# A two-layer transformer block in fp32: ScalarE and GpSimd kept in the order of issue during attention, the settling of a chunk split into parts, and three PSUM banks of small pieces in one ring

## The chip, the cores and the metric

The kernel runs on one core of a Trainium2 chip. The metric is the time of one execution on the device, in microseconds. A core has five engines that run side by side, each with an instruction stream of its own: TensorE (PE in the profile; PEld is its loading of weights), VectorE (DVE), ScalarE (ACT), GpSimd (POOL) and SyncE (SP), which here only issues DMA transfers. GpSimd issues the indirect DMAs (gathers and scatters by a list of rows). Matmul results land in PSUM, which has eight banks of 128 x 512 fp32; everything else on the chip lies in SBUF. An engine takes its instructions in the order of its stream, and semaphores tell it when another engine's or a DMA's result is there.

## The reference, cut to what matters

Eight sequences of 256 tokens, 512 wide, all in fp32:

```
x  = hidden_states                                  # 8 x 256 x 512
xn = layernorm(x)
x  = x + lightning_attention(xn) + moe(xn)          # layer 0
xn = layernorm(x)
x  = x + softmax_attention(xn) + low_rank_moe(xn)   # layer 1

lightning_attention: qkv = silu(xn @ qkv_w.T), 32 heads of 128;
    scores = q k^T * decay (causal), o = scores v; o scaled by its RMS over all heads, times norm_w,
    gated by sigmoid(xn @ gate_w.T), then @ out_w.T
moe: 16 experts, the best 2 of each token (chosen in 2 of 4 groups), weighted by their scores,
    each silu(x w1 + b1) * (x w2 + b2) @ w3 + b3; two shared experts for every token
softmax_attention: one head of 128
low_rank_moe: 64 experts of rank 16, the best 16 of each token, gates by softmax
```

## The kernel before, in words

**Tiling.** The 2048 tokens are four chunks of 512 (NCH), each of four tiles of 128 tokens (TPC). All large products use a seven-product Strassen scheme (p1 to p7), with sums of weights and tokens made beforehand.

**The opening** normalizes, runs the shared experts, routes and lays out the slots of the chosen experts. It takes the first 195 us or so, and uses other functions than the ones changed.

**Attention.** In the pool `attn`, for each chunk i = 0 to 3 and each of eight groups of four heads g, the seven products of the scheme run one after another (`Outer`, L964, one for each of `plan`), and each of these is split by the same scheme once more: p1, p7, p3 of the Outer before, p6, p4, p2, p5. So a group makes 7 x 7 = 49 small products (in chunk 0, which also writes the weight sums for later, 7 x 8 without the inner saving). A group with its chunk is called a unit here; there are 32, and in the even stretch from 1529.12 to 1969.10 us six of them take 73.3 us each. One `product` (L662, its matmul is L667) is four matmuls into a quarter of a PSUM bank each, eight records in the trace. The banks of these products are ps_a (2), ps_b and ps_e. A finished bank is copied by ScalarE to cp (`copied`, L997), or combined by VectorE to r, c or a (`result`, through `tt`, L97); GpSimd adds r into c. When a quarter of a unit is complete, `Quarter.begin` books the small pieces that use it: silu of q and k (L745), the gate (L750 to L752), scores (L770, L771, into ps_sc), attend (L782, L783, into ps_o; squares for the RMS at L797; gated outputs gT at L802), and the output projection (L859, or `project_plain`, L879), whose results are added into acc.

**Slots.** After each product `slot()` (L680) takes the next piece that is due from a list; `later(n, f)` books a piece n slots ahead. One slot runs one piece, or two if more than twelve wait; pieces that give TensorE nothing to do are not counted.

**Experts.** In the units from the ninth on, `expert(j)` books 47 blocks of 128 expert slots, three to a unit for seven units and then two. Each starts with a load of its tokens by SP (xw from xd) and a gather of its weights by GpSimd (L698), and has turn (L707), up (L717, into ps_sc; h at L724, he at L725) and down (L729, into ps_y; copied to ye at L734, stored to yd) 8, 11 and 14 slots later. The tokens were scattered to xd (L1095) during chunk 0.

**Small PSUM pieces.** ps_sc has two banks that take turns, ps_y one bank, ps_o one. A piece can write a bank once the reader of what it last held is done.

**Settling.** `settle` (L552) brings a chunk from layer 0 to layer 1: for each of the two experts of a token it gathers four tiles of rows from yd (L559, GpSimd) and adds them, times the gate, into x (L566, VectorE), then normalizes (L231 to L236). Chunk 0 is settled at the unit before the last of chunk 3 (`wrapped_up`, L1146), the others in the tail.

**The tail.** Layer 1 runs for each chunk: low_rank(0) (L1416, matmuls at L1423) with the turning of the softmax and its product with v as fillers, settle of the next chunk, low_rank(2) with the attention output as filler (`attended`, L1465, into ps_y), then a last `seven` (L1493) with route, qk, values, softmax and gates of the next chunk's head as fillers, after turn_rows (L240).

**Who sets the order.** The program is traced in Python, and a scheduler of the language then orders the stream of each engine by priorities and its own estimates. So an instruction can run ahead of one that was traced before it, if no data stand against it.

Of the kernel before, what the change touches and what calls it, by code (L numbers as in the profile page):

```python
# [9 lines left out]
FP = mybir.dt.float32  # L10
# [8 lines left out]
P = 128  # L19
CH = 512  # L20
NCH = NT // CH
TPC = CH // P
# [11 lines left out]
TOP = 2  # L34
# [3 lines left out]
NSLOT = NMT * P  # L38
# [28 lines left out]
def block_kernel(  # L67
# [25 lines left out]
    nc = tc.nc  # L93
    mm = nc.tensor.matmul

    def tt(o, a, b, op, eng=None):
        (eng or nc.vector).tensor_tensor(o, a, b, op)  # L97
# [8 lines left out]
    ps = ctx.enter_context(tc.tile_pool(name="ps", bufs=1, space=PSUM))  # L106
# [21 lines left out]
        return stage.tile([P, C + WROW], FP, tag="xw", name=name)  # L128

    def ps_sc():  # L130
        return ps.tile([P, 512], FP, tag="sc", name="ps_sc", bufs=2)

    def ps_o():
        return ps.tile([P, 512], FP, tag="o", name="ps_o", bufs=1)

    def ps_y():
        return ps.tile([P, 512], FP, tag="y", name="ps_y", bufs=1)


    opening = ExitStack()  # L140
# [26 lines left out]
    for i in range(1, NCH):  # L167
# [8 lines left out]
    yd = dram.tile([NSLOT, C], FP, name="yd")  # L176
# [27 lines left out]
        out=before, in_=before, pattern=[[1, E], [-1, E]], compare_op=ALU.is_gt,  # L204
# [11 lines left out]
        out=dist[:, 0:S], in_=dist[:, 0:S], pattern=[[1, S]], compare_op=ALU.is_ge,  # L216
# [134 lines left out]
    def add(o, a, b, eng=None):  # L351
        tt(o, a, b, ALU.add, eng)
# [70 lines left out]
    for i in range(NCH):  # L423
# [23 lines left out]
    slots = const.tile([P, TOP, NTT], I32, name="slots")  # L447
    slot_gates = const.tile([P, TOP, NTT], FP, name="slot_gates")
# [6 lines left out]
        out=earlier, in_=earlier, pattern=[[1, P]], compare_op=ALU.is_gt,  # L455
# [25 lines left out]
    at = NTT * E  # L481
# [67 lines left out]
    settled = {}  # L549
    accs = []  # L550

    def settle(i, x_, spare):  # L552


        for n in range(TOP):
            y = spare()
            for t in range(TPC):
                at = i * TPC + t
                nc.gpsimd.indirect_dma_start(  # L559
                    out=y[:, t, :], out_offset=None, in_=yd[:, :],  # L560
                    in_offset=bass.IndirectOffsetOnAxis(ap=slots[:, n, at : at + 1], axis=0),
                    bounds_check=NSLOT - 1, oob_is_err=False,
                )
            for t in range(TPC):
                gate = slot_gates[:, n, i * TPC + t : i * TPC + t + 1]
                nc.vector.scalar_tensor_tensor(  # L566
                    x_[:, t, :], y[:, t, :], gate, x_[:, t, :], ALU.mult, ALU.add
                )
        xn = spare()
        normalize(xn, x_)  # L570
        return xn

    acc = {}

# [12 lines left out]
    def finish(i, r):  # L587

        for b in range(2):
            for t in range(2):  # L590
                n = 2 * b + t
                o = r[:, n, :].rearrange("p (h c) -> p h c", h=2)
                nc.vector.scalar_tensor_tensor(
                    o, acc[i][:, 2 * b : 2 * b + 2, t], all_rms[i][:, n : n + 1], o, ALU.mult, ALU.add
                )

    def spare8():
        return staged("spare")[:, 0 : TPC * C].rearrange("p (t c) -> p t c", t=TPC)

    with tc.tile_pool(name="attn", bufs=1) as attn:  # L600
        sums_ = {}


# [72 lines left out]
        def later(after, f):  # L676
            pieces.append((now[0] + after, len(pieces), f))
            pieces.sort(key=lambda x: x[:2])

        def slot():  # L680

            now[0] += 1
            n = 0
            while pieces and pieces[0][0] <= now[0] and n < (2 if len(pieces) > 12 else 1):
                f = pieces.pop(0)[2]
                f()
                n += getattr(f, "func", f).__name__ not in ("silu", "gate", "row", "scatter", "load_sum", "sums1", "sums2", "sums3", "sums4", "out_sum")


        class Expert:  # L690
# [270 lines left out]
        class Outer:  # L961
# [10 lines left out]
            x_ = {}  # L972
# [173 lines left out]
        def wrapped_up():  # L1146

            x_, y = spare8(), spare8()
            nc.sync.dma_start(out=x_, in_=xs_[0])
            accs.append(x_)  # L1150
            settled[0] = settle(0, x_, lambda: y)

        def prepare(n):
            if n < len(plan):
# [120 lines left out]
    def spare():  # L1275
        return work.tile([P, TPC, C], FP, tag="spare", name="spare")

    def next_x(i):
        x_ = spare8() if i % 2 == 0 else work.tile([P, TPC, C], FP, tag="x", name=f"x{i}", bufs=1)
        accs.append(x_)  # L1280
        if i + 1 < NCH:
            nc.sync.dma_start(out=x_, in_=xs_[i])
        else:
            nc.sync.dma_start(out=x_, in_=xr[i])
            finish(i, x_)
        return x_
# [104 lines left out]
    for i in range(NCH):  # L1391
# [24 lines left out]
        def low_rank(j, fill):  # L1416

            gates2 = [spread(h * HJ + j) for h in range(2)]

            def product(bank, w, xx, first):  # L1420
                for n in range(2):
                    for c in range(HC):
                        mm(  # L1423
                            bank[:, bass.ts(n, S)], w[:, c, bass.ts(j + n, P)], xx[:, c, :],
                            start=(first and n == 0 and c == 0), stop=(c == HC - 1),
                            skip_group_check=True,
                        )

            def out_(h, b, bank, c):
                o = hg[:, h * HJ + j : h * HJ + j + 2, bass.ts(b, S)]  # L1430
                if c is not None:
                    add(c, bank, c)
                    bank = c
                tt(o, bank.rearrange("p (n s) -> p n s", n=2), gates2[h][:, :, bass.ts(b, S)], ALU.mult)

            seven(work, product, WA, XA, out_, fill)
# [28 lines left out]
        def attended(t):  # L1465
# [2 lines left out]
            mm(py, oT[:, bass.ts(t, P)], wo_t, start=True, stop=True)  # L1468
            add(xc[:, t, :], py, xc[:, t, :])

        low_rank(0, {2: [partial(turned, 0)], 7: [partial(turned, 1)], 5: [partial(weighed, 0)], 3: [partial(weighed, 1)]})
        if i + 1 < NCH:
            settled[i + 1] = settle(i + 1, next_x(i + 1), spare)
        low_rank(2, {k: [partial(attended, t)] for t, k in enumerate((2, 7, 5, 3))})
        if i + 1 < NCH:
            if i % 2:
                yT1 = xT[0]
            else:
                yT1 = work.tile([P, NC, CH], FP, tag="yT", name=f"yT{i + 1}", bufs=1)
# [123 lines left out]
```

## Time and profile before

| | |
|---|---|
| median of 3 runs | 2904.78 us (2901.41 to 2913.6) |
| the profiled execution | 2910.55 us |
| its span | 2908.9 us |
| its mean granted TensorE clock | 0.989 |
| TensorE busy | 2811.0 us, 97% of the span |
| VectorE busy | 1553.3 us, 53% |
| ScalarE busy | 953.1 us, 33% |
| GpSimd busy | 1469.4 us, 51% |
| moved by DMA | 763.20 MB, 262 GB/s in the mean |

In stretches (the stage borders are rounded; busy time of TensorE, mean granted clock):

| stretch, us | what runs | PE busy, us | clock |
|---|---|---|---|
| 0 to 195 | opening | 167.31 | 0.92 |
| 195 to 850 | attention, chunk 0 | 639.66 | 0.99 |
| 850 to 1430 | chunk 1, experts | 568.44 | 1.00 |
| 1430 to 2021 | chunk 2, experts | 585.59 | 1.00 |
| 2021 to 2240 | chunk 3, last experts | 215.68 | 1.00 |
| 2240 to 2600 | chunk 3, chunk 0 settled | 342.26 | 0.98 |
| 2600 to 2909 | tail, layer 1 | 292.02 | 0.99 |

How to read a group or a wait: the line of the kernel, the engine, the operation, then output<-input by the program's names; ps_ names are PSUM banks. A wait names the instruction that stood still, what released it, the microseconds in total, how often and the longest. "c", "r", "acc" and other results of L97 come from one helper for all elementwise operations of two tensors, so they are told apart by name, not by line. A row of the timeline has start, length, engine, line, operation and, in brackets, how long the engine was idle before it and what ended that.

### The profile page before, as it was taken

How to read it: one execution, taken by the hardware profiler on the slowest of the kernel's cores; microseconds unless marked ns; L12 is line 12 of the kernel's file. 1: busy time of each engine (PE TensorE's matmuls, PEld its weight loads, DVE VectorE, ACT ScalarE, POOL GpSimd, SP SyncE). 2: the span in 40 equal slices, each digit the busy share in tenths (PEclk: the TensorE clock that was granted, in tenths of full speed). 3: DMA queues.
4: the chain of work that ended last, by engine and by line, in shares of the span. 5: the costliest groups of instructions: out<-in, count | busy, mean ns of one | idle time of the engine just before them, and what ended most of it. 6: DMA issues, size and time to landing. Idle time of an engine off the chain costs nothing.

```text
span 2908.9 us, 49460 instructions
## 1 busy us (share of the span) xinstructions
PE 2811.0 (97%) x19864; PEld 2570.9 (88%) x19864; DVE 1553.3 (53%) x2615; ACT 953.1 (33%) x1683; POOL 1469.4 (51%) x1213
## 2 busy tenths in 40 slices
PE   8989999999999999999999999999999989999999
PEld 4469999999989999999999999999999979987877
DVE  7555666666544545444545555555445455558463
ACT  3312222221244333333443333333433334332111
POOL 4535666565445555555645555445444665554110
PEclk9999999999999999999999999999999999999999
DMA  7788998888987777777777777777777776653111
GB/s 263 291 307 329 350 350 344 342 333 329 368 319 258 277 251 262 260 264 277 285 263 258 257 259 260 261 280 282 282 257 257 282 297 225 224 213 96 60 60 60
DMA packets 161942, 763.20 MB, mean 262 GB/s; under 512 B 18209, under 2 KB 24225, under 8 KB 109874
## 3 DMA queue, kind: packets, MB, share of 16 engines
q1 hardware_dynamic: 149826, 706.25, 65.7%
q0 software_dynamic: 11888, 53.79, 5.3%
q8 instruction: 157, 2.57, 0.4%
q14 instruction: 71, 0.58, 0.1%
HBM read 596.14 MB, written 163.05 MB: 261 GB/s over the span
## 4 chain that ended last, share of the span: by engine, by line
PE 78%; DVE 9%; DMA 4%; issue 4%; POOL 2%; ACT 1%; SPq 0%; DVEq 0%; POOLq 0%; ACTq 0%
PE ps_a L667 22%; PE ps_e L667 11%; PE ps_b L667 7%; PE ps_y L859 5%; PE ps_sc L859 4%; PE ps_o L782 3%; PE ps_sc L770 3%; PE ps_sc L717 2%; PE ps_y L879 2%; PE ps_sc L879 2%; DVE c L97 2%; PE ps_a L1493 2%; PE ps_o L783 2%; PE ps_sc L771 2%; PE ps_y L729 1%
## 5 line engine op out<-in xcount | busy, mean ns | idle before, releaser
L667 PE MATMUL ps_a<-xt,w 128*128 128x128 f32 x5376 | 752.9, 276 | 15.0 <-DVE r L97 7.4
L667 PEld LDWEIGHTS ps_a<-xt,w 128*128 128x128 f32 x5376 | 683.1, 193 | 36.4 <-issue 14.9
L97 POOL TENSOR_TENSOR c<-c,r 128x512 f32<-128x512 f32 x240 | 323.7, 1366 | 186.3 <-DVE r L97 138.7
L745 ACT ACTIVATE c<-c 128x512 f32<-128x512 f32 x256 | 161.3, 630 | 656.7 <-DVE c L97 360.2
L667 PE MATMUL ps_e<-xt,w 128*128 128x128 f32 x2688 | 374.3, 275 | 2.0 <-DVE c L97 1.3
L97 POOL TENSOR_TENSOR c<-c 128x512 f32<-128x512 f32 x216 | 270.7, 1269 | 184.6 <-DVE c L97 182.6
L97 POOL TENSOR_TENSOR w<-w 128x512 f32<-128x512 f32 x224 | 292.9, 1322 | 133.4 <-DVE w L97 67.8
L667 PEld LDWEIGHTS ps_e<-xt,w 128*128 128x128 f32 x2688 | 344.7, 192 | 12.4 <-issue 4.1
L97 POOL TENSOR_TENSOR sums<-sums,sq 128x512 f32<-128x512 f32 x120 | 154.3, 1286 | 386.5 <-ACT sq L797 386.1
L667 PE MATMUL ps_a<-w,xt 128*128 128x128 f32 x1792 | 346.9, 275 | 0.0
L997 ACT COPY cp<-ps_a 128x512 f32<-128x512 f32 x336 | 195.0, 580 | 426.9 <-PE ps_a L667 426.9
L667 PEld LDWEIGHTS ps_a<-w,xt 128*128 128x128 f32 x1792 | 272.6, 192 | 0.0
L97 DVE TENSOR_TENSOR c<-ps_a,c 128x512 f32<-128x512 f32 x232 | 158.0, 687 | 214.5 <-PE ps_a L667 213.5
L667 PE MATMUL ps_b<-xt,w 128*128 128x128 f32 x1680 | 236.3, 277 | 4.8 <-ACT c L1011 4.2
L802 DVE SCALAR_TENSOR_TENSOR gT<-ps_o,nw,c 128x256 f32<-128x256 f32 x256 | 111.9, 479 | 226.5 <-ACT sq L797 222.4
L667 PEld LDWEIGHTS ps_b<-xt,w 128*128 128x128 f32 x1680 | 216.9, 194 | 16.1 <-issue 5.5
L859 PE MATMUL ps_y<-wo,gT 128*128 128x256 f32 x736 | 175.4, 381 | 0.6 <-DVE acc L97 0.6
L667 PE MATMUL ps_e<-w,xt 128*128 128x128 f32 x896 | 173.5, 275 | 0.0
L770 PE MATMUL ps_sc<-c 128*128 128x256 f32 x512 | 154.1, 383 | 11.3 <-DVE he L725 7.7
L97 DVE TENSOR_TENSOR s<-ps_sc,decay 128x384 f32<-128x384 f32 x256 | 139.1, 551 | 39.0 <-PE ps_sc L771 37.7
L782 PE MATMUL ps_o<-s,c 128*128 128x256 f32 x512 | 153.8, 382 | 4.3 <-DVE s L97 4.2
L859 PEld LDWEIGHTS ps_y<-wo,gT 128*128 128x128 f32 x736 | 132.8, 190 | 15.5 <-issue 0.7
(307 smaller groups left out, 4768.1 us busy)
## 6 DMA issues: line engine op xcount, KB each, us to landing
w<-in_w_att_dram SPq DMA_DIRECT2D x128, 1024.0 KB
st<-in_w_att_dram SPq DMA_DIRECT2D x32, 1024.0 KB
wo<-in_w_out_dram SPq DMA_DIRECT2D x113, 256.0 KB
decay<-dec SPq DMA_DIRECT2D x64, 384.0 KB
w<-ws0p SPq DMA_DIRECT2D x12, 1792.0 KB
w<-ws1p SPq DMA_DIRECT2D x12, 1792.0 KB
w<-ws2p SPq DMA_DIRECT2D x12, 1792.0 KB
w<-ws3p SPq DMA_DIRECT2D x12, 1792.0 KB
```

Of the source, the lines that this page charges most:

```text
L97: (eng or nc.vector).tensor_tensor(o, a, b, op)
L667: mm(bank[:, bass.ts(ty, P)], a, b, start=(first and ty == 0), stop=True, skip_group_check=True,)
L717: mm(pu[:, bass.ts(n, P)], w12[:, n, c, :], self.xeT[:, c, :], start=(c == 0), stop=(c == NC - 1),)
L745: nc.scalar.activation(qk, qk, AF.Silu)
L770: mm(p[:, 0:S], self.c[:, 2 * hh, P : 2 * P], q, start=True, stop=True)
L771: mm(p[:, S : S + P], self.c[:, 2 * hh + 1, P : 2 * P], q[:, 1, :], start=True, stop=True,)
L782: mm(po[:, bass.ts(hh, S)], v[:, 0, :], self.s[:, hh, 0:S], start=True, stop=False)
L783: mm(po[:, hh * S + P : (hh + 1) * S], v[:, 1, :], self.s[:, hh, S:], start=False, stop=True,)
L802: nc.vector.scalar_tensor_tensor(gT[:, h, :].rearrange("p (t n) -> p t n", t=2), po[:, bass.ts(h, S)].rearrange("p (t n) -> p t n", t=2), ...
L859: mm(py[:, bass.ts(t, S)], self.O[p][:, hh, bass.ts(t, P)], self.wo[p][:, hh, :], start=(t == 0 and hh == 0), stop=(hh == 1), skip_group_c ...
L879: mm(py[:, bass.ts(h, S)], gT[:, hh, bass.ts(t, P)], self.wo[pair, h][:, hh, :], start=(h == 0 and hh == 0), stop=(hh == 1), skip_group_ch ...
L997: nc.scalar.copy(c, bank)
```

## The change

It has three parts.

1. During attention (the pool `attn`), the streams of ScalarE and GpSimd are kept in the order in which the program is traced. The other engines are ordered by the scheduler as before.
2. `settle` becomes `gather(i, n, y)`, which issues four gathers for one expert choice n, and `settle(i, n, x_, y)`, which adds them; the four additions keep their place in program order on VectorE. Normalization is called apart. For chunk 0: the gathers of n = 0 are issued where settle stood; 16 slots later the additions, then the gathers of n = 1 into the same buffer; another 16 slots on, their additions and the normalization, into that buffer. In the tail: both sets of gathers of the next chunk go ahead of low_rank(0) into two buffers, the additions behind low_rank(0), the normalization behind low_rank(2). The two new pieces count among those that give TensorE nothing.
3. ps_sc has three banks instead of two, and ps_y takes one of these instead of a bank of its own. The sum stays at eight banks.

```diff
     def ps_sc():
-        return ps.tile([P, 512], FP, tag="sc", name="ps_sc", bufs=2)
+        return ps.tile([P, 512], FP, tag="sc", name="ps_sc", bufs=3)
...
     def ps_y():
-        return ps.tile([P, 512], FP, tag="y", name="ps_y", bufs=1)
+        return ps_sc()
...
-    def settle(i, x_, spare):
-        for n in range(TOP):
-            y = spare()
-            for t in range(TPC):
-                at = i * TPC + t
-                nc.gpsimd.indirect_dma_start(
...
-            for t in range(TPC):
-                gate = slot_gates[:, n, i * TPC + t : i * TPC + t + 1]
+    def gather(i, n, y):
+        for t in range(TPC):
+            at = i * TPC + t
+            nc.gpsimd.indirect_dma_start(
+                out=y[:, t, :], out_offset=None, in_=yd[:, :],
...
+    def settle(i, n, x_, y):
+        for t in range(TPC):
+            gate = slot_gates[:, n, i * TPC + t : i * TPC + t + 1]
+            tc.keep_in_program_order(
                 nc.vector.scalar_tensor_tensor(
                     x_[:, t, :], y[:, t, :], gate, x_[:, t, :], ALU.mult, ALU.add
                 )
-        xn = spare()
-        normalize(xn, x_)
-        return xn
+            )
...
-    with tc.tile_pool(name="attn", bufs=1) as attn:
+    with tc.tile_pool(name="attn", bufs=1) as attn, tc.manual_schedule(engines={mybir.EngineType.Activation, mybir.EngineType.Pool}):
...
-                n += getattr(f, "func", f).__name__ not in ("silu", "gate", "row", "scatter", "load_sum", "sums1", "sums2", "sums3", "sums4", "out_sum")
+                n += getattr(f, "func", f).__name__ not in ("silu", "gate", "row", "scatter", "load_sum", "sums1", "sums2", "sums3", "sums4", "settle0", "settle1", "out_sum")
...
-            settled[0] = settle(0, x_, lambda: y)
+            settled[0] = y
+            def settle0():
+                settle(0, 0, x_, y)
+                gather(0, 1, y)
+            def settle1():
+                settle(0, 1, x_, y)
+                normalize(y, x_)
+            gather(0, 0, y)
+            later(16, settle0)
+            later(32, settle1)
...
+        following = []
+        if i + 1 < NCH:
+            following = [next_x(i + 1), spare(), spare()]
+            for n in range(TOP):
+                gather(i + 1, n, following[1 + n])
         low_rank(0, {2: [partial(turned, 0)], 7: [partial(turned, 1)], 5: [partial(weighed, 0)], 3: [partial(weighed, 1)]})
-        if i + 1 < NCH:
-            settled[i + 1] = settle(i + 1, next_x(i + 1), spare)
+        for n, y in enumerate(following[1:]):
+            settle(i + 1, n, following[0], y)
         low_rank(2, {k: [partial(attended, t)] for t, k in enumerate((2, 7, 5, 3))})
+        if following:
+            settled[i + 1] = spare()
+            normalize(settled[i + 1], following[0])
```

More of the change, by code (lines that the diff above doesn't have):

```diff
@@ L550, in block_kernel @@
     accs = []
-    def settle(i, x_, spare):
-        for n in range(TOP):
-            y = spare()
-            for t in range(TPC):
-                at = i * TPC + t
-                nc.gpsimd.indirect_dma_start(
[L560 to L563, printed above, removed]
-            for t in range(TPC):
-                gate = slot_gates[:, n, i * TPC + t : i * TPC + t + 1]
+    def gather(i, n, y):
[3 more added lines that the diff above has]
+                out=y[:, t, :], out_offset=None, in_=yd[:, :],
+                in_offset=bass.IndirectOffsetOnAxis(ap=slots[:, n, at : at + 1], axis=0),
+                bounds_check=NSLOT - 1, oob_is_err=False,
+            )
[3 more added lines that the diff above has]
+            tc.keep_in_program_order(
                 nc.vector.scalar_tensor_tensor(
@@ L568, in settle @@
                 )
-        xn = spare()
-        normalize(xn, x_)
-        return xn
+            )
     acc = {}
```

## The prediction, made before the changed kernel ran

> **What bounds the kernel now.** I read the busy times first, then the chain, then the waits of TensorE, then stretches of the run.
>
> The page, its first part and its chain:
>
> ```profile
> PE 2811.0 (97%) x19864; PEld 2570.9 (88%) x19864; DVE 1553.3 (53%) x2615; ACT 953.1 (33%) x1683; POOL 1469.4 (51%) x1213
> PE 78%; DVE 9%; DMA 4%; issue 4%; POOL 2%; ACT 1%; SPq 0%; DVEq 0%; POOLq 0%; ACTq 0%
> ```
>
> TensorE is busy for 97% of the span and no other engine passes 53%, so the change can win only where TensorE stands still or runs at a lower clock. ScalarE and GpSimd matter as releasers. The waits of TensorE (what waited, for whom, us in total, times, longest):
>
> ```profile
> PE ps_sc L859 <- DVE gT L802: 7.8, 1, 7.8
> PE ps_sc L770 <- DVE he L725: 7.7, 7, 3.2
> PE ps_a L667 <- DVE r L97: 7.4, 15, 1.5
> PE ps_y L729 <- DVE acc L97: 5.8, 6, 1.0
> ...
> PE ps_y L1468 <- DVE spare L97: 4.0, 2, 2.3
> PE ps_y L729 <- ACT acc L867: 3.8, 3, 1.5
> ...
> PE ps_sc L770 <- DVE acc L97: 3.2, 1, 3.2
> PE ps_e L1423 <- DVE cp L97: 2.8, 2, 1.7
> ```
>
> No wait is large; the whole stock of them is some 100 us, and a good part lies in the opening (before 195 us), which the diff doesn't touch. One place has several of them: the settling of chunk 0, near 2375 to 2409 us. There the stretches (us, then each engine's busy time, granted clock, DMA share, GB/s) are:
>
> ```profile
> 2378.00:2383.00 5.00, 3.70 (x16) 3.17 (x16) 5.00 (x6) 0.00 (x0) 4.14 (x4) 0.66 0.67 212
> 2383.00:2390.00 7.00, 5.83 (x40) 5.08 (x40) 6.32 (x6) 2.09 (x4) 5.80 (x6) 1.00 0.82 290
> 2390.00:2397.50 7.50, 0.00 (x0) 0.00 (x0) 1.92 (x4) 0.00 (x0) 0.28 (x1) 0.67 0.38 134
> 2397.50:2403.00 5.50, 5.46 (x17) 4.70 (x18) 5.46 (x14) 4.43 (x7) 3.21 (x3) 0.52 0.08 21
> ```
>
> and VectorE's own order in it:
>
> ```profile
> 2376.65 0.75 DVE L566 SCALAR_TENSOR_TENSOR spare<-spare,slot_gates 128x512 f32<-128x512 f32 x1 [6.99 <-DMA spare<-yd,slots]
> ...
> 2378.85 2.92 DVE L566 SCALAR_TENSOR_TENSOR spare<-spare,slot_gates 128x512 f32<-128x512 f32 x1
> ...
> 2382.89 3.91 DVE L566 SCALAR_TENSOR_TENSOR spare<-spare,slot_gates 128x512 f32<-128x512 f32 x2
> ...
> 2395.29 0.75 DVE L566 SCALAR_TENSOR_TENSOR spare<-spare,slot_gates 128x512 f32<-128x512 f32 x1 [5.97 <-DMA spare<-yd,slots]
> ...
> 2397.00 0.87 DVE L802 SCALAR_TENSOR_TENSOR gT<-ps_o,nw,c 128x256 f32<-128x256 f32 x2
> ```
>
> The eight additions of settling stand in VectorE's order ahead of attention's work and wait there for the gathered rows: 6.99 us, then 5.97 us. The gated outputs gT (L802) come behind them, and TensorE's L859 waits 7.83 us for these.
>
> **Part 1, the bank ring.** No instruction is added or removed. Two banks of small pieces and one for ps_y become a ring of three. A piece then waits for the reader of the third bank before it, whatever its kind, where a ps_y piece used to wait for the reader of the last ps_y and a ps_sc piece for the last but one. The waits for a bank's reader are L770 on he 7.7 and on acc 3.2, L729 on acc 5.8 and 3.8, and L1468 on spare 4.0: 24.5 us. One more allocation of distance is about one or two products, and a product of eight matmul records is 0.89 us; the mean wait is 24.5/19 = 1.3 us. So most go. Not all: down (L729) also needs he, its own operand. At 957.70 it started after 0.97 us, and he was there at 957.05, so about two thirds of the 9.6 us of L729 goes, 6.4. Of L770 10.9 I take 8.5 (of the two waits of 3.2 us a third stays), of L1468 all 4.0; slower records after these two gaps (1.36 us for two instead of 1.12) add little. Sum: 6.4 + 8.5 + 4.0 = 18.9. Bounds: 27 with everything and the clock, 8 if a ps_sc piece now meets the slower readers of ps_y (the ye copy on ScalarE, the acc additions) that had been kept apart.
>
> **Part 2, the order of issue on ScalarE and GpSimd.** The instructions are the same, 453 of ScalarE's 1675 and 214 of GpSimd's 1224 change places, hardly any of TensorE's. What ScalarE waits for, of all waits:
>
> ```profile
> ACT c L745 <- DVE c L97: 360.2, 159, 13.6
> ACT c L745 <- POOL c L97: 273.0, 71, 16.0
> DVE he L725 <- ACT h L724: 106.2, 44, 4.5
> ```
>
> Today silu (L745) is put ahead of h (L724) and of the bank copies (L997) while it waits for GpSimd. An example: silu waited until 955.78, h ran at 956.32, two copies behind that. In the issue order h and the copies stand ahead of it. It touches the he waits, which part 1 has counted, and the r waits (7.4 us, 15 times), where r needs a bank copy. I take 3 of these 7.4 and 1 of the 1.1 us for L667 on cp: 4 us. Bounds: 9 if the whole of r goes; 0 if r is late through VectorE alone.
>
> On GpSimd the moved steps have DMAs. The scatters of the first chunk stop coming in pairs (60.9 us of its waiting is for the previous scatter), which hides nothing TensorE waits for: 0. The weight gathers of the experts (L698) come later. They go today as soon as the buffer's last reader (down) is done, 14 to 67 us ahead of up (L717). In the issue order each stands behind the additions traced before it. For one of them, GpSimd has today:
>
> ```profile
> 1007.81 1.01 POOL L698 DMA_INDIRECT xw<-in_w_exp_dram,rows__1106  x1 [1.12 <-DMA w<-in_w_att_dram]
> ...
> 1041.74 1.26 POOL L97 TENSOR_TENSOR gT<-gT 128x512 f32<-128x512 f32 x1
> ```
>
> and its up starts at 1059.58. In the new order it follows the gT addition that ends at 1043.0: 1059.58 - 1043.0 - 1.0 for the instruction leaves 15.6 us. Worked so for all 47, 40 have 14 to 21 us, six have 11.4 and one 9.9. The landing of these gathers, from all of their issues:
>
> ```profile
> DMA to landing us min/median/max: 5.6/8.2/13.0
> ```
>
> At the median nobody waits; at the maximum the six would wait 1.6 us each and the one 3.1, 13 in sum. I take 2 us of loss, bounds 0 and 13. SP's order hardly moves (65 of 1004); the xw loads from xd on SP stay where they were.
>
> **Part 3a, chunk 0 settled in parts.** The stall costs: the five waits of TensorE between 2375 and 2409 us, 2.36 + 1.32 + 0.86 + 7.83 + 0.57 = 12.9, and the lower clock behind two of them, (1 - 0.66) x 3.70 + (1 - 0.52) x 5.46 = 3.9 by the stretches: 16.8 us. Here the Trainium skill's rule (TensorE: Matmul & The Clock Gate, Part 1) would say half the clock for about 3.4 us after an idle window of about 3.4 us: that is 1.7 us behind the 7.83 wait, and nothing behind the 2.36 one, 14.6 in all. The rows show 0.66 behind the 2.36 us wait and 0.52 for 5.5 us behind the long one, so I take 16.8.
>
> In the new form a gather has 16 slots before its additions. A unit of 73.3 us has 7 x 7 = 49 products, a slot each: 1.5 us, so 24 us, against a landing of the L559 gathers of 8.9 us at most. The waits for rows are gone. What stays is that four pinned additions hold VectorE in one go, twice. Alone one takes 0.75 us, so 3 us. But the rule that speaks against the change is in the Trainium skill (SBUF — State Buffer, "Who interferes with whom"): a VectorE instruction with two SBUF inputs and a GpSimd instruction that reads SBUF block each other for the whole instruction. By it each of the eight could wait for one GpSimd addition of 1.27 to 1.37 us: 4 x 2.05 = 8.2 us per group. The rows agree in part: 2.92 us for one and 3.91 for two while GpSimd worked, 0.75 at 2395.29 while it was idle. The five from 2378.85 to 2388.7 took 2.92 + 3.91 + 1.40 = 8.2, a mean of 1.65; I take this, 6.6 us per group. Behind them queue the bank additions (c, r, acc) and gT; TensorE has some 3 to 4 us of other products before it needs them, so about 3 us per group are left over, 6 in all. Gain: 16.8 - 6 = 11; by the rule at its full price 16.8 - 2 x 4.7 = 7.4, by the lone row 16.8. The second gather waits in GpSimd's order for the first four additions (write after read), with attention's c additions queued behind it; these have about 10 us before a silu needs them: 0, up to 3.
>
> **Part 3b, the tail.** Three times the gathers stand ahead of low_rank(0), the additions between the two low_rank calls, the normalization behind the second. The gathers have some 15 us of products as cover for 8.9. The eight additions are 8 x 0.74 = 5.9 us in one go on VectorE, with GpSimd nearly idle; the next bank that needs VectorE is used again 10 to 14 us later, so 0. The normalization now ends just ahead of turn_rows: 3.6 us of VectorE and ScalarE work after the last product against 3.45 us of p1 of the next seven; up to 1 us each, 2 taken. The L1423 waits of 2.8 may go: 2. Sum 0, bounds +4 (gain) and -6.
>
> **The sum.** 18.9 + 4 - 2 + 11 + 0 = 31.9 us. The profiled execution took 2910.55 us (span 2908.9 and 1.65 around it): 2878.6. It lay 0.2% above the median of the runs, 2904.78, so by ratio 2872.9. Rounded: 2872.
>
> **The rivals.** (a) *The waits only change their name.* TensorE leaves one bank's wait and meets the next reader on VectorE: r, he as an operand. For it: L667 on r comes 15 times in the same places, and VectorE is the releaser of nearly all. Against it: from 1500 to 2000 us TensorE already runs at 99%, so a unit without these waits exists. Then a third of part 1, nothing of part 2, and part 3a at 11 with 2 lost on the gathers: 6 + 11 - 2 = 15: about 2890. (b) *More goes than the listed waits*, with the long form of 3a at full gain, all of r and the tail's 4: 27 + 9 + 16.8 + 4 = 57: about 2848. (c) *Slower: the weight gathers come too late.* Place: up, L717, in units 8 to 27. Price: 47 experts times the excess of landing over slack. The gathers run beside other weight loads (DMA share 0.74), and a landing of 16 to 17 us instead of 8.2 on most of them makes 47 x 1.1 = 52 us, less the 34 of the rest: 2922. It decides at 34/47 = 0.7 us of excess on each. Against it: the longest landing so far is 13.0. (d) *No change*, if the pinned additions and the fixed order of GpSimd take back what the rings give: 3a at the rule's 7.4, the gathers at 13 and the tail at -6 leave 18.9 + 4 + 7.4 - 13 - 6 = 11: about 2894.
>
> **Numbers.** A difference under 0.5% (14.5 us) can't be told from no change here. Chances: the forecast (2858 to 2882) 0.50, (a) 0.18, (b) 0.12, (d) 0.10, (c) 0.10. Faster by over 0.5% means under 2890.3: the forecast, (b) and somewhat over half of (a): 0.73. Within it: the rest of (a), (d) and a little of (c): 0.18. Slower: 0.09. The range takes in (b)'s end and (d): 2846 to 2908, with (c) and a little of (b) outside.
>
> **What would show it.** No PE wait over 3 us near the settling of chunk 0 and a granted clock of 1.00 there; L770 on he and L729 on acc near zero; L1468 gone from the list; the ScalarE waits at L745 no smaller, but he waits shorter; landing of L698 still near 8 us and no wait of L717. Wrong it would be if L717 waits for xw, if L667 on r grows by what L770 and L729 lose, if four additions of L566 (L567 in the new numbering) take over 8 us, or if turn_rows (L243) waits over 1 us for the normalization.

## The result, and the profile after

The changed kernel takes 2859.09 us in the median of 6 runs (2852.31 to 2864.06). The kernel before, run beside it, takes 2909.93 us (6 runs). The ratio is 0.983, with a 95% interval of 0.9804 to 0.9856: 1.7% faster, clear of noise. Run again later it gave 2857.73 against 2905.47, a ratio of 0.9843 (0.9818 to 0.9867). The forecast was 2872 with a range of 2846 to 2908, and it held; but the gain was some 48 to 51 us, half as much again as the 32 of the working.

The first part of the page of the changed kernel, span 2854.4 us, and its waits of TensorE (what waited, for whom, us in total, times, longest). Attention's lines have moved up by one, those of the tail down by 11 to 19:

```profile
PE 2796.7 (98%) x19864; PEld 2566.1 (90%) x19864; DVE 1569.7 (55%) x2615; ACT 948.2 (33%) x1683; POOL 1465.7 (51%) x1213
```

```profile
PE ps_a L666 <- DVE r L97: 7.7, 17, 1.7
...
PE ps_sc L243 <- DVE spare L236: 2.6, 4, 0.8
PE ps_b L666 <- DVE mv L232: 2.6, 1, 2.6
...
PE ps_sc L858 <- POOL gT L97: 1.8, 1, 1.8
```

L770 on he and acc, L729 on acc, L1468 on spare and the 7.8 us of L859 on gT are gone. L667 on r (now L666) is what it was. Three larger entries are new: on mv and on gT from GpSimd, both in the new settling of chunk 0, and L243 on spare, which is turn_rows in the tail waiting for the late normalization.

**Lost time by stage.** To compare runs I add up, over all records of TensorE in a stage, by how much the next one starts later than the usual spacing of its kind (0.112 us for a record of 128 columns, 0.216 for 256, 0.429 for 512). This holds the waits and the records slowed by a lower clock. The stages are cut at the same count of records in each run, those of the kernel before at 195, 850, 1430, 2021, 2240 and 2600 us; a stage is good to about 1 us (a second execution of the changed kernel differs from the first by at most 0.8 in any of them; a spacing a little too long gives a small negative), and the opening, which no edit touches, moves by some 5.

The medians stand beside medians of the kernel before of 2903 to 2910 us in their own groups. A row of stages is one execution, whose time can lie some us from the median: the row of the kernel before took 2910.55 us, that of the ring alone 2882.25, that of the pinned c 2839.89. So differences of stages say where time went, and medians say how much.

| run | opening | chunk 0 | chunk 1 | chunk 2 | chunk 3, experts | chunk 3, settling | tail | sum | median us |
|---|---|---|---|---|---|---|---|---|---|
| before | 39.7 | 23.3 | 15.4 | 7.9 | 4.5 | 26.1 | 17.5 | 134.5 | 2904.78 |
| after | 38.4 | 11.6 | 1.3 | 4.5 | 2.3 | 10.1 | 11.4 | 79.6 | 2859.09 |
| ring alone | 39.2 | 14.2 | 5.7 | 5.7 | 2.7 | 20.8 | 17.5 | 105.9 | 2888.49 |
| order alone | 39.6 | 13.1 | 2.4 | 5.4 | 2.9 | 24.4 | 14.5 | 102.4 | 2879.87 |
| settling in parts alone | 38.8 | 21.4 | 14.0 | 8.0 | 4.5 | 11.5 | 15.1 | 113.2 | 2888.23 |
| ring and order | 39.6 | 10.3 | 1.3 | 4.5 | 2.3 | 23.6 | 17.5 | 99.0 | 2878.58 |
| order and settling | 43.9 | 13.2 | 2.4 | 5.4 | 3.1 | 10.0 | 16.6 | 94.5 | 2874.98 |
| ring and settling | 39.7 | 16.5 | 5.7 | 6.5 | 3.7 | 11.8 | 8.0 | 91.9 | 2868.74 |
| after, pinned c | 39.7 | 7.9 | -0.9 | -0.6 | 0.3 | 6.3 | 11.0 | 63.8 | 2846.76 |
| the same, settled tile by tile | 42.1 | 8.2 | -1.5 | -0.6 | 0.3 | 0.5 | 10.3 | 59.4 | 2834.43 |

The table's 134.5 - 79.6 = 54.9 agrees with the difference of the two spans, 54.5. So the time came from waits and clock, not from less work.

**The settling of chunk 0** in the changed kernel, GpSimd and then VectorE:

```profile
2389.85 1.03 POOL L556 DMA_INDIRECT spare<-yd,slots  x1
...
2396.05 1.26 POOL L97 TENSOR_TENSOR gT<-gT 128x512 f32<-128x512 f32 x1
```

```profile
2407.98 2.55 DVE L567 SCALAR_TENSOR_TENSOR spare<-spare,slot_gates 128x512 f32<-128x512 f32 x2
...
2411.06 1.82 DVE L567 SCALAR_TENSOR_TENSOR spare<-spare,slot_gates 128x512 f32<-128x512 f32 x2
...
2436.31 2.73 DVE L567 SCALAR_TENSOR_TENSOR spare<-spare,slot_gates 128x512 f32<-128x512 f32 x4
```

No addition waits for its rows any more. What is left of the stall has two causes. Four gathers in one go keep GpSimd from 2389.85 to 2394.8, the sum gT behind them is late, and L858 waits 1.8 us. And the last four additions and the statistics of the normalization stand on VectorE in one go, so that ps_b is read late, behind mv: 2.6 us.

### The profile page after: what moved, and what is told of

Read it like the earlier page. It is cut to its first block, busy times and chain, and to the rows that moved or that the text cites. A ratio compares the mean times of both kernels' runs of the same rounds, so it can differ in the third digit from the quotient of the medians.

```text
span 2854.4 us, 49572 instructions
## 1 busy us (share of the span) xinstructions
PE 2796.7 (98%) x19864; PEld 2566.1 (90%) x19864; DVE 1569.7 (55%) x2615; ACT 948.2 (33%) x1683; POOL 1465.7 (51%) x1213
## 5 line engine op out<-in xcount | busy, mean ns | idle before, releaser
L666 PE MATMUL ps_a<-xt,w 128*128 128x128 f32 x5376 | 750.9, 276 | 11.7 <-DVE r L97 7.7
L666 PEld LDWEIGHTS ps_a<-xt,w 128*128 128x128 f32 x5376 | 681.9, 192 | 30.1 <-issue 14.3
L666 PE MATMUL ps_e<-xt,w 128*128 128x128 f32 x2688 | 373.4, 275 | 1.3 <-DVE c L97 1.3
L666 PEld LDWEIGHTS ps_e<-xt,w 128*128 128x128 f32 x2688 | 344.4, 192 | 11.2 <-issue 3.8
L666 PE MATMUL ps_a<-w,xt 128*128 128x128 f32 x1792 | 346.7, 275 | 0.0
L858 PE MATMUL ps_sc<-wo,gT 128*128 128x256 f32 x1288 | 305.1, 379 | 1.8 <-POOL gT L97 1.8
L97 DVE TENSOR_TENSOR acc<-ps_sc,acc 128x512 f32<-128x512 f32 x208 | 143.3, 690 | 265.8 <-PE ps_sc L858 198.8
L666 PEld LDWEIGHTS ps_a<-w,xt 128*128 128x128 f32 x1792 | 272.3, 192 | 0.0
L858 PEld LDWEIGHTS ps_sc<-wo,gT 128*128 128x128 f32 x1288 | 232.3, 190 | 26.8 <-POOL gT L97 2.0
L666 PE MATMUL ps_b<-xt,w 128*128 128x128 f32 x1680 | 236.4, 277 | 6.8 <-ACT c L1010 4.2
L666 PEld LDWEIGHTS ps_b<-xt,w 128*128 128x128 f32 x1680 | 217.3, 194 | 17.5 <-issue 8.2
L744 ACT ACTIVATE c<-c 128x512 f32<-128x512 f32 x256 | 148.9, 627 | 170.1 <-DVE c L97 170.0
L796 ACT ACTIVATE sq<-ps_o 128x512 f32<-128x512 f32 x120 | 71.6, 597 | 382.3 <-PE ps_o L782 382.3
L666 PE MATMUL ps_e<-w,xt 128*128 128x128 f32 x896 | 173.2, 275 | 0.0
```

The source lines that it names most:

```text
L666: mm(bank[:, bass.ts(ty, P)], a, b, start=(first and ty == 0), stop=True, skip_group_check=True,)
L744: nc.scalar.activation(qk, qk, AF.Silu)
L796: nc.scalar.activation(sq, po, AF.Square)
L858: mm(py[:, bass.ts(t, S)], self.O[p][:, hh, bass.ts(t, P)], self.wo[p][:, hh, :], start=(t == 0 and hh == 0), stop=(hh == 1), skip_group_c ...
```

## The experiments

Each kernel takes parts of the change away or adds to it; all compute the whole block.

**The three parts one by one.** *The ring alone:*

```diff
-        return ps.tile([P, 512], FP, tag="sc", name="ps_sc", bufs=2)
+        return ps.tile([P, 512], FP, tag="sc", name="ps_sc", bufs=3)
-        return ps.tile([P, 512], FP, tag="y", name="ps_y", bufs=1)
+        return ps_sc()
```

> The kernel before with the ring of three banks alone; the scheduler still orders ScalarE and GpSimd, and settling is as before. Theory (each part removes its own waits): L770 on he and acc, L729 on acc and L1468 on spare leave the list of TensorE's waits, 24.5 us with some slow records behind them, so 22 to 28 us less than before (-0.8 to -1.0%); the stall at the settling of chunk 0 stays at 15 us or more. Rival (the order of ScalarE is what frees the he waits): L770 on he stays at 5 us or more and the gain is 10 to 16 us.

Measured: 2888.49 us against 2905.7, ratio 0.994 (0.9916 to 0.9963), 17 us less. The waits on L770, on acc and on spare left the list; down now waits for its own operand:

```profile
PE ps_e L1423 <- DVE cp L97: 7.9, 2, 5.7
...
PE ps_sc L729 <- DVE he L725: 4.1, 8, 1.6
```

The gain lies below the theory's 22 to 28. L1423 on cp, grown from 2.8 to 7.9 us in the tail, can account for some 5 us of that; the rest is not traced, for the profiled execution, at 2882.25 us among the fastest of its eight, loses 28.6 us less than the one before. In attention up to the settling (chunk 0 to the last experts) the lost time fell from 51.1 to 28.3.

*The order alone:*

```diff
-    with tc.tile_pool(name="attn", bufs=1) as attn:
+    with tc.tile_pool(name="attn", bufs=1) as attn, tc.manual_schedule(engines={mybir.EngineType.Activation, mybir.EngineType.Pool}):
```

> The kernel before with the order of issue on ScalarE and GpSimd alone. Theory: it shortens only waits that the ring removes as well; L729 on acc and L1468 on spare stay, r waits stay at 7 to 8 us: 2 to 8 us less than before. Rival: the order alone removes the he waits and the two waits of 3.2 us in chunk 0, and the gain is 12 us or more. A third possibility: with GpSimd's gathers of settling in program order and not split, the stall at chunk 0's settling moves or grows, and the time is above that of before.

Measured: 2879.87 us, ratio 0.9913 (0.9886 to 0.9941), 26 us less. My theory fell. With ps_y still alone in its bank, L729 on acc is not in the list at all, nor is L770 on he; in attention up to the settling 51.1 us fell to 23.8, more than by the ring. Of the third possibility one half came true: the stall of the settling moved. ScalarE's row, and TensorE's:

```profile
2415.97 0.30 ACT L223 ACTIVATE rstd<-mv,eps_t 128x4 f32<-128x4 f32 x1 [22.33 <-DVE mv L232]
```

```profile
2416.79 1.65 PE L667 MATMUL ps_a<-xt,w 128*128 128x128 f32 x6 [18.91 <-ACT cp L997]
```

In the order of issue the square root of the normalization waits 22.33 us on ScalarE for statistics of rows whose gathers GpSimd issues only from 2394.84 us on, and the bank copies stand behind it. The stall has another form but about the same size (the stage loses 24.4 us, 26.1 before), so the order alone leaves this part of the time where it was.

*The settling in parts alone* (the changed kernel with the two diffs above undone):

> The kernel before with the settling in parts alone (gathers apart, pinned additions, late normalization). Theory: the stall near 2375 to 2409 us goes but for 5 us, and the tail changes by less than 4: 10 to 16 us less than before (-0.35 to -0.55%); L770, L729 and L1468 as before. Rival (the order on GpSimd is needed for the gathers to come early): the scheduler still puts gathers and additions elsewhere, and under 5 us are gained.

Measured: 2888.23 us, ratio 0.9931 (0.9909 to 0.9953), 17.5 us less, a little over the theory. The stage of the settling fell from 26.1 to 11.5; the others moved by 2.4 or less. The early gathers, the pinned additions and the late normalization were not taken apart.

**Two parts at a time.** *Ring and order, settling in one piece:*

> The changed kernel without the settling in parts: ring and order together, settle in one piece. Theory: the bank waits gone as in the ring alone, a few us from the order on top: 26 to 34 us less than before; the settling of chunk 0 still costs 12 us or more. Rival (the parts work only together): under 20 us, with a larger settling stall than before, since the eight gathers now stand in one block in GpSimd's order.

Measured: 2878.58 us, ratio 0.9906 (0.9879 to 0.9934), 27 us less, as the theory had it, with L667 on cp at 18.2 us in one wait. Ring and order alone gave 17 + 26 = 43 us, so here they share 16. All three parts alone gave 60.5, all together 48 to 51.

*Order and settling, no ring:*

> The changed kernel with ps_y back in a bank of its own and two banks of ps_sc: order and settling in parts, no ring. Theory A (silu ahead of h on ScalarE holds he, he holds VectorE, and acc behind it comes late, so the order alone cures the waits of L770 and L729): only L1468 on spare comes back, some 4 to 6 us, so 2862 to 2868 us or a ratio of 0.984 to 0.987 to the kernel before. Theory B (the prediction: the ring's distance takes 18.9 us of waits): 2875 us or more, ratio 0.989 or above, with L729 on acc back in the list.

Measured: 2874.98 us against 2903.43, ratio 0.99 (0.9887 to 0.9914). The number is theory B's, the sign is theory A's: L729 on acc did not come back. Against the changed kernel's first profile the lost time is 14.9 us higher, of which 5.5 in the opening, 5.2 in the tail (L1479 on spare 3.1 is back) and 4.4 in attention up to the settling. So neither theory holds whole; with the order in place the ring is worth little in attention, and some 5 us in the tail. The 5.5 of the opening are not the ring's: the order alone, with the same banks, has 39.6 there. By the medians, order and settling together (28 us) also stay below their sum of 43, although the stage of the settling fell by 14.4 as it should; the opening and the tail took 4.3 and 2.1 of that back, and for the rest no cause was found.

*Ring and settling, no order:*

> The changed kernel without the order of issue: ring and settling in parts, ScalarE and GpSimd as the scheduler orders them. Theory A (ring and order cure the same waits): down waits for he 3 to 5 us, the rest of attention's waits as in the ring alone, so 10 to 15 us more than the changed kernel beside it (about 2872). Theory of the prediction (order adds only 4 us to the ring): 2 to 6 us more.

Measured: 2868.74 us against 2857.73 of the changed kernel beside it, 11 us more, within theory A. Down waits for he 4.1 us in 8 places, and attention up to the settling loses 32.4 us instead of 19.7.

**Do ring and order share?** In attention up to the settling they do. From the kernel before, the ring takes off 22.8 us of lost time, the order 27.3 and both 32.7, so 17.4 are shared; with the settling in parts throughout it is 15.5, 23.8 and 28.2, so 11.1. Over the whole run the medians show it in the first set alone (16 us). In the second, the ring adds 19 us, the order 11 and both 30 to 33, and nothing seems shared. The medians of the groups carry intervals of some 4 to 8 us to each side, and the opening and the tail differ between these kernels too, so the size of the shared part stays open.

**Which engine's order.**

```diff
-engines={mybir.EngineType.Activation, mybir.EngineType.Pool}
+engines={mybir.EngineType.Activation}
```

> The changed kernel with only ScalarE kept in the order of issue; GpSimd is ordered by the scheduler. Theory A: ScalarE's order is the cure, so he on h stays short and the time is within 6 us of the changed kernel (ratio 0.981 to 0.986). Rival: GpSimd's order is needed too, for additions that silu waits for come late, ScalarE's copies wait behind these silus, and L667 on cp appears with over 5 us: ratio 0.988 or more.

Measured: 2860.19 us, ratio 0.9849 (0.983 to 0.9868), about the changed kernel's time. With GpSimd alone in the set:

> The changed kernel with only GpSimd kept in the order of issue; ScalarE is ordered by the scheduler. Theory A: down (L728) waits for he again as in the ring alone, some 3 to 6 us, and bank copies wait behind a silu that waits; ratio 0.986 to 0.990. Rival: GpSimd's order brings the additions earlier, no silu waits long, and the time is that of the changed kernel within 3 us.

Measured: 2865.7 us, ratio 0.988 (0.9864 to 0.9896), within theory A's 0.986 to 0.990, and no better than ring and settling with no order at all (0.9886). The intervals of the two just touch, so the times alone would not decide. The waits of he on h (all engines' list), ScalarE's order alone and then GpSimd's alone:

```profile
DVE he L724 <- ACT h L723: 71.2, 41, 3.9
```

```profile
DVE he L724 <- ACT h L723: 107.1, 44, 4.5
```

The first is the changed kernel's (71.1), the second that of the kernel before (106.2). So it is ScalarE's order that frees he. The chain behind it can be read in the rows of ScalarE and VectorE in the kernel before:

```profile
955.78 0.63 ACT L745 ACTIVATE c<-c 128x512 f32<-128x512 f32 x1 [7.65 <-POOL c L97]
956.32 0.35 ACT L724 ACTIVATE h<-ps_sc,xw 128x128 f32<-128x128 f32 x1
```

```profile
956.70 0.35 DVE L725 SCALAR_TENSOR_TENSOR he<-ps_sc,xw,h 128x128 f32<-128x128 f32 x1 [4.54 <-ACT h L724]
956.97 0.68 DVE L97 TENSOR_TENSOR acc<-ps_y,acc 128x512 f32<-128x512 f32 x1
```

ScalarE has a silu ahead of h that waits for GpSimd; he waits 4.54 us for h with VectorE standing still; and acc, whose product ended at 955.8, waits behind he in VectorE's order. Its lateness is what kept the one bank of ps_y, and TensorE's L729, waiting. This is no single case. Followed back in the same way, 25 of the 44 late he in the kernel before have a silu directly ahead of their h, with 70.9 of the 106.2 us, and all six waits of L729 on VectorE's acc come behind one of them. In the changed kernel silu has one entry left among the waits, 40 times, and none for GpSimd:

```profile
ACT c L744 <- DVE c L97: 170.0, 40, 12.8
```

All 41 late he there wait for the product up itself. The chain does not cover every wait that went: the 3.2 us of L770 on acc lie at 583 us, before the first expert. The ring cures the chain at its end, by another bank, and the order at its head. In chunk 1, where 13 of the 25 places lie and all six of these waits of L729, the lost time (with the ring and the settling in parts) is 5.7 us with no order, 10.0 with GpSimd's alone, 2.1 with ScalarE's alone and 1.3 with both. With GpSimd's alone down waits there 2.6 us for he and TensorE 2.4 for bank copies; with ScalarE's alone neither is in the list.

**The wait that stayed.** The wait on r is the largest one left in attention. In the changed kernel, VectorE and GpSimd near one of its places (TensorE starts again at 1584.78):

```profile
1580.93 0.69 DVE L97 TENSOR_TENSOR r<-ps_e,cp 128x512 f32<-128x512 f32 x1 [1.15 <-PE ps_e L666]
1581.72 1.80 DVE L97 TENSOR_TENSOR c<-c,r 128x512 f32<-128x512 f32 x1
1583.44 0.68 DVE L97 TENSOR_TENSOR r<-ps_b,cp 128x512 f32<-128x512 f32 x1
1584.05 0.67 DVE L97 TENSOR_TENSOR r<-ps_a,cp 128x512 f32<-128x512 f32 x1
```

```profile
1581.70 1.27 POOL L97 TENSOR_TENSOR c<-c,r 128x512 f32<-128x512 f32 x1 [3.19 <-DVE r L97]
```

GpSimd's c<-c,r and VectorE's start together, both released by the r before. VectorE's takes 1.80 us where an r of the same size takes 0.69, and the next two r stand behind it. The edit collects these additions and pins them behind the last r:

```diff
-                        add(c_, c_, r)
+                        held_sums.append(partial(kept_add, c_, r))
+                        if (i, j) != (1, 0) and (i, j) != (0, 0):
+                            flush()
...
+        def kept_add(o, r):
+            tc.keep_in_program_order(nc.vector.tensor_tensor(o, o, r, ALU.add))
+        def flush():
+            while held_sums:
+                held_sums.pop(0)()
...
+                flush()
                 ye = attn.tile(
```

> The changed kernel with VectorE's additions c<-c,r (of p7) collected and pinned behind the r of the same Outer, so that no addition of two SBUF operands stands between two r. Theory: the r waits of TensorE, 7.7 us in 17 places (10.5 with the slower records behind them), come from c<-c,r, which takes 1.8 us instead of 0.7 while GpSimd adds, and which stands ahead of the last r: they fall below 2 us and the time by 6 to 10 us against the changed kernel (ratio to the kernel before 0.980). Rival: r is late for other reasons (the copy cp, the gated outputs), and the waits stay at 7 us.

Measured: 2846.76 us, ratio 0.9806 (0.9792 to 0.9821). TensorE's waits on r are gone from the list, all of them, and VectorE's rows show why:

```profile
1576.25 0.69 DVE L97 TENSOR_TENSOR r<-ps_a,cp 128x512 f32<-128x512 f32 x1
1576.86 4.86 DVE L692 TENSOR_TENSOR c<-c,r 128x512 f32<-128x512 f32 x3
```

The three additions still take 1.6 us each, but nothing that TensorE needs stands behind them. The gain over the changed kernel is 11 to 12 us between medians and 7 to 11 by the ratios, so at or just above the theory's 6 to 10; the two were not run side by side. (The profiles differ by 15.8 us of lost time, but this one is the fastest of its five executions.)

The same run tells whether GpSimd is the cause of the 1.80 us. The next of these additions meets no instruction of GpSimd, whose rows here end at 1581.17 and begin again at 1583.93:

```profile
1582.11 0.68 DVE L692 TENSOR_TENSOR c<-c,r 128x512 f32<-128x512 f32 x1
```

```profile
1575.29 5.88 POOL L97 TENSOR_TENSOR c<-c,r 128x512 f32<-128x512 f32 x4 [3.18 <-DVE r L97]
1583.93 2.52 POOL L97 TENSOR_TENSOR c<-c,r 128x512 f32<-128x512 f32 x2 [2.76 <-DVE r L97]
```

Of the 96 such additions in this run 15 meet none, and they take 0.67 to 0.68 us; the other 81 take 1.55 in the mean. An r, one of whose operands lies in PSUM, takes at most 0.69 whether GpSimd adds or not.

**A faster version.** On top of this, chunk 0 is settled tile by tile, and in the tail the normalization moves ahead of the last product of low_rank(2):

```diff
+            for t in range(TPC):
+                later(1 + 2 * t, partial(gather0, t))
+                later(16 + 2 * t, partial(settle0, t))
+                later(32 + 2 * t, partial(settle1, t))
+                later(44 + 2 * t, partial(scaled, t))
...
-        low_rank(2, {k: [partial(attended, t)] for t, k in enumerate((2, 7, 5, 3))})
+        low_rank(2, {2: [partial(attended, 0)], 7: [partial(attended, 1)], 5: [partial(attended, 2)], 3: [partial(attended, 3), normalized]})
```

> The changed kernel with the pinned c<-c,r of the run before, and the settling of chunk 0 one tile at a time (gather, addition, statistics and scaling each in slots of their own), and in the tail the normalization of the next chunk as a filler ahead of the last product of low_rank(2). Theory: the waits on mv 2.6 and on gT from GpSimd 1.8, which come from four gathers or four additions and statistics in one go, vanish, and L243 on spare falls from 2.6 to under 1: 4 to 7 us less than with the pinned additions alone, so 18 to 24 us less than the changed kernel beside it. Rival: single additions meet GpSimd's additions as often, and the waits only move; no gain over the pinned additions (10 to 16 us less than the changed kernel).

The changed kernel ran beside it, unaltered:

> The changed kernel again, unaltered, beside the three others of this group. All theories: a ratio of 0.981 to 0.986 to the kernel before, and the same waits of TensorE as in its first profile (r 7.7 us, mv 2.6, gT from GpSimd 1.8), within 1 us each.

Measured: 2834.43 us, ratio 0.9755 (0.9732 to 0.9779), against 2857.73 of the changed kernel (0.9843): 23 us less, within the theory. The waits on mv and on gT from GpSimd vanished, and the stage of the settling loses 0.5 us, where the changed kernel loses 10.1 and the pinned additions alone 6.3. What it adds to the pinned additions was forecast as 4 to 7 us; the lost time has 4.4 less, the medians, from different groups, 12. The normalization's move did little: L243 on spare is 2.6 us, where 3.0 stands in the run beside it, not under 1 as expected. The unaltered kernel repeated its waits within 1 us each (r 7.8, mv 2.6, gT from GpSimd 1.8).

**The rival that did not come.** The slower side of the forecast was that the experts' weights come too late. In the changed kernel they land in 6.9 to 13.0 us, median 7.5, and no up waits for them. To find the edge, the gathers are issued four slots later:

```diff
+                later(4, self.load)
+            def load(self):
                 nc.gpsimd.indirect_dma_start(
                     out=self.we, out_offset=None, in_=w_exp[:, :],
```

> The changed kernel with the weight gathers of the experts issued four slots later (some 6 us), all else as before. From its trace, up starts 12.0 to 12.4 us behind the issue for nine experts and 15 to 22 us for 38; the landings take 6.9 to 13.0 us, median 7.5. Theory: with 6 us less the nine wait 1 to 2 us each and those of the others with a long landing 2 to 3 us: L716 waits for the gather by 10 to 30 us in sum, and the time grows by as much (ratio to the changed kernel 1.003 to 1.010). Rival: landings become shorter or the slots stretch with them, and it costs under 5 us.

Measured: 2874.59 us, ratio 0.9897 (0.9875 to 0.9919), 16.9 us more than the changed kernel beside it, as the theory had it.

```profile
PE ps_sc L719 <- DMA xw<-in_w_exp_dram,rows__1106: 12.2, 4, 4.4
```

These four waits hold most of it, and slower records follow. (A wait of 4.6 us at the weight load of one up is the same stall as its matmul's, at 816.17 us, and not more.) So the order of issue left these gathers less than four slots of room; how much less was not run.

## Why the prediction was right, point by point

**The total.** Range and direction held, the range being wide; the sum was too small. It was 31.9 us; between the two profiles it was 54.5, between medians 48 to 51. By the stages of the table: attention up to the settling lost 31.4 us less, where the working had 14.9 of part 1 (without the tail's 4.0), 4 of part 2 and -2 for the gathers, 16.9; the settling 16.0, where it had 11; the tail 6.1, where it had the 4.0 of L1468.

**Part 1, the ring.** 18.9 was forecast and 17.2 measured when the ring stands alone. The remark that down also needs he was right: 4.1 us of this wait were left, where the working had left 3.2 of L729's 9.6. That the two figures lie so close is in part luck: by the stages the ring took 22.8 us from attention, where the working had 14.9, and 5.3 from the settling, where it had none, but nothing from the tail, where it had 4.0 and L1423 gave back 5.1. And what the working took for the cause, too small a distance between banks, was for most of these waits only the last link of the chain.

**Part 2, the order: the term that was mis-sized.** The step read that the order touches the he waits "which part 1 has counted" and is worth 4 us of r and cp. Measured: 26 us alone, with a stall of 18.9 us in place of the old waits of 12.9 in the settling, and 11 us on top of ring and settling. Two things were wrong in it. The waits on r did not fall (7.4 before, 7.7 after): they come from VectorE's own order, as the lower bound of that step had it. And with the order in place the third that part 1 had to leave, he as an operand, goes as well, and so do waits of chunk 0 that I had not put into the sum. The he row, 106.2 us and 44 times, stood in my own excerpt; I read it as a part of L770, and did not follow VectorE behind he, where acc is. One of the signs failed with it: the waits of silu, which were to be no smaller, fell from 360.2 + 273.0 us to 170.0.

**The gathers of the experts.** Forecast -2, measured no wait. The slack that the working had (14 to 21 us for 40, 11.4 for six, 9.9 for one, from the end of the instruction) was 12.0 to 12.4 from the issue for nine and 15 to 22 for the others; the late version shows that such a loss is real when the slack shrinks by four slots.

**Part 3a.** The residue was forecast as 6 us and measured as 1.8 on gT, 2.6 on mv and slower records behind the latter (a granted clock of 0.72 from 2441 to 2447 us). Size right, cause wrong, so the match is luck: the eight additions took 2.55 + 1.82 + 2.73 = 7.1 us, 0.89 each, not 1.65. Of the two prices weighed there, the rule's (each held by a whole GpSimd addition) was too high, for the second four met no GpSimd addition; the first four, with GpSimd adding, took 4.37, 1.09 each. The step that called the gathers' effect on GpSimd's other work 0, up to 3, is where the 1.8 us belong. In the tail the additions took 0.74 each, as forecast.

**Part 3b.** Forecast 0, measured some 2 us of gain beyond L1468's. L1423 on cp is 2.8 us before, 1.8 after, 7.9 with the ring alone and 9.1 with ring and order, though no part of the change was made for it; what decides it stays open. The late normalization cost about what was set down for it: L243 on spare waits 2.6 us in four places, where the working had 2. That is over the 1 us that was named as a sign of being wrong, and the total bore it.

**The clock.** Behind the wait of 7.83 us in the kernel before I had taken the measured rows, not the shorter half-rate of the rule weighed there; the settling stage fell by 16.0, where the rows gave 16.8 for the stall and 6 for the residue. Too many small waits share that stage to tell 3.9 us of clock from 1.7 by it.

**The rivals.** (a), that waits only change their name, is refuted: r did not take over what the others lost (7.4 before, 7.7 after). (b), that more goes than the listed waits, is in the time as near as the forecast (11 us off against 13) and in the gain nearer: 57 us, against 48 to 51 measured and 32 forecast. Its way was partly another, for r stayed. (c) did not come; gathers issued four slots later brought 16.9 us of it. (d) fell.

## What to carry to other kernels

When several waits on one engine name different banks and readers, look at what stands ahead of each late reader in its own engine's stream: here a silu on ScalarE made he late, he made VectorE stand still, and acc behind it kept a bank. A cure at the head of such a chain and one at its end need not add up (here 43 us apart and 27 together, without the third part), so measure each part alone and with each of the others. And an order of issue is only as good as the pieces: a long piece that waits for a DMA, in one block, can stall whatever stands behind it in the kept order: here ScalarE for 22.33 us, and TensorE behind its copies for 18.91.

## What the runs showed of the hardware

An addition of 128 x 512 on VectorE with both operands in SBUF takes 0.68 us where GpSimd does nothing meanwhile (15 of 96 with the pinned c), 1.55 in the mean where the two overlap, and 1.80 in the row where they start together; with one operand in PSUM it takes 0.69 in either case. In the changed kernel, where all 96 c<-c,r on VectorE overlap with GpSimd, their mean is 1.52 us. This agrees with the rule of the Trainium skill that was weighed above (SBUF — State Buffer, "Who interferes with whom"); the price, 0.87 us in the mean, is less than a whole GpSimd addition of 1.27. What the runs show besides is that such an addition costs TensorE nothing where it stands behind the work that others wait for, and 7.7 us of listed waits where it stands ahead of it.

The clock dropped behind short waits too: the wait on mv of 2.6 us in the changed kernel was followed by a granted clock of 0.72 over 6 us, while the wait of 1.8 on gT left it at 1.00. The six records behind the 18.91 us wait took 1.65 us instead of 0.83.
